# Layer 1 of a four-layer scan network: delta·u·B by plain multiplies for two of four pairs of states

## The chip, the core and the metric

The kernel runs on one core of a Trainium2 chip. The metric is the device time of one execution in microseconds (us). The engines have the short names of the profile: PE is TensorE, DVE is VectorE, ACT is ScalarE, POOL is GpSimd, and SP is the queue that issues most DMAs. All data are 32-bit floats.

## What is computed

The reference applies four layers to an image batch x of shape (4, 64, 64, 192). Only layer 1 is touched by the change. It runs four "mamba" blocks: over rows, rows reversed, columns, columns reversed. Each block treats every line of 64 pixels as a sequence of its own, with 384 channels d and 16 states n:

```
u      = silu(conv1d(in_proj(x)))                  # 4 taps, along the line
dt,B,C = x_proj(u)                                 # B, C: 16 values a pixel
delta  = softplus(dt_proj(dt) + bias)
h      = exp(delta * A[d,n]) * h + delta * u * B[n]     # along the line, h = 0 at its start
y[d]   = sum over n of h * C[n]
out    = out_proj((y + u * D) * silu(z))
```

Layers 0 and 3 are scans of the same kind over whole images, with a state carried on; layer 2 is a Toeplitz product by matmuls.

## The kernel before

**Chunks and units.** Layer 1 is cut into 128 jobs ("chunks"): 4 directions, 4 images, 8 chunks of T = 512 pixels (8 lines). A chunk has 384 channels, which are 6 groups g of 64, and 16 states, which are 4 pairs p: a tile of 128 partitions holds 64 channels twice, for the lower and the upper 8 states, and 2 x 512 columns hold two states of each half. So a unit (t, p, c) with g = 2t + c covers 64 channels and four states in one tile of 128 x 1024, and a chunk has 24 units: three tiles t, each with the eight (p, c) of the list `TWO` (L29).

**One unit.** `feed` (L304) makes the two inputs of the scan two units ahead (`AHEAD` = 2): delta·u·B, and dA = exp(delta·A) by two activations on ACT (L347). `scan` (L350) runs one `tensor_tensor_scan` on DVE (L357), and POOL multiplies h by C (L369) into hc. `collect` (L372) sums over states on PE by a matmul with `fold`, two units (c = 0 and 1) at a time, into y. When the last pair of a tile has been collected, `add` (here `gated`, L762) does y + uD on DVE and the product with z on POOL.

**delta·u·B in two ways.** For most units PE forms it: the transposed delta·u (`dtuT`) is the weight, and the moving operand is a set of diagonal matrices that carry B; eight matmuls (sixteen records in the trace) a unit at L324 write a PSUM tile b. The diagonals of one pair are 16 activations of 128 x 128 on ACT (L282), spread over four steps. Units listed in `direct`, in layer 1 both c of pair 3, need no diagonals: `spread` (L291) multiplies delta·u (tile `dtu2`) by a broadcast B (tile `bbc`) on POOL, three units ahead (`EARLY` = 3), into bs in SBUF (one buffer). For such a unit dA goes into the PSUM tile b instead of a fixed SBUF tile, and a copy (L335) first sets the start of each line in it to zero. PSUM has two buffers of b, so the work of `feed` for unit i + 2 that writes b waits for the scan of unit i.

**Order.** `run_jobs` (L104) emits, for each unit i, `feed` of i + 2, `scan` of i, `spread` of i + 3, one waiting `collect`, and then the steps that are due at i. The steps of a later chunk's preparation are placed by hand in `when` and `steps` (L784 to L789), counted in units from that chunk's start; minus 24 is one chunk earlier. So in the middle of a chunk's 24 units ACT has its table switches for `input_of` (L738, silu of u), `gate` (L752, silu of z) and `finish` (softplus) of later chunks. `plan` (L146) places the loads: tiles c (broadcast C), `bbc`, `both` (delta) and `dtu2` are fetched 12 units before their first use, or, where the buffer is still in use, a few units after its last one (`behind`: 2 in layer 1); diagonals 10 units before, or 3 after. A C tile is kept for a whole chunk, for all three t. The framework that lowers the program may shift instructions of one engine against each other, so the queues follow this order only roughly.

Of the kernel before, what the change touches and what calls it, by code (L numbers as in the profile page):

```python
# [7 lines left out]
F32 = mybir.dt.float32  # L8
# [11 lines left out]
T = 512  # L20
# [10 lines left out]
LAST = 2  # L31
LEAD = 12
LEAD_DIAG = 10
D1, PD, KD = 576, 96, 6
# [2 lines left out]
class Kernel:  # L37
# [66 lines left out]
    def run_jobs(self, jobs, pools):  # L104


        G = jobs[0]["DI"] // 64
        order = []
        for t in range(-(-G // 2)):
            order += [(t, *one) for one in (TWO if 2 * t + 1 < G else ONE)]  # L110
        units = [(k, *one) for k in range(len(jobs)) for one in order]
        per = len(order)
        steps = {}
        for k, job in enumerate(jobs):
            for at, step in self.prepare(job, pools) + job["steps"]:
                steps.setdefault(k * per + at, []).append(step)
        for at, load in self.plan(jobs, order, pools):
            steps.setdefault(at, []).append(load)
        start, end = min(steps), max(len(units) + 3, max(steps) + 1)
        waiting = []  # L120
        for i in range(min(start, -EARLY), end):
            if 0 <= i + AHEAD < len(units):
                k, t, p, c = units[i + AHEAD]
                self.feed(jobs[k], t, p, c, pools)
            todo = waiting[:1]
            if 0 <= i < len(units):
                k, t, p, c = units[i]
                self.scan(jobs[k], t, p, c, pools)
            if 0 <= i + EARLY < len(units):
                k, t, p, c = units[i + EARLY]  # L130
                if c in jobs[k]["direct"].get(p, ()):
                    self.spread(jobs[k], t, p, c, pools)
            if 0 <= i < len(units):
                if (i + 1) % 2 == 0:
                    waiting += [(units[i][0], [one[1:] for one in units[i - 1 : i + 1]], n) for n in range(2)]


            if todo:
                k, two, n = waiting.pop(0)
                self.collect(jobs[k], two, n, pools)  # L140
                if n and two[1][1] == LAST:
                    jobs[k]["add"](two[0][0])
            for step in steps.get(i, []):
                step()

    def plan(self, jobs, order, pools):  # L146


        uses, ready = {}, {}
        for k, job in enumerate(jobs):  # L150
            job["cbc"], job["bbc"], job["diag"], job["both"], job["dtu2"] = {}, {}, {}, {}, {}
            when = {name: k * len(order) + at for name, at in job["when"].items() if isinstance(at, int)}

            near = 2 if job["carry"] is not None else 5
            dtu = when["finish"] + 3 if job["carry"] is not None else when["store"] + 5
            for j, (t, p, c) in enumerate(order):
                i, g = k * len(order) + j, 2 * t + c
                direct = c in job["direct"].get(p, ())
                reads = [("c", p, i, when["project"] + 5), ("both", g, i - AHEAD, when["finish"] + near)]
                if direct:  # L160
                    reads += [("bc", p, i - EARLY, when["project"] + 5), ("dtu2", g, i - EARLY, dtu)]
                else:
                    reads.append(("diag", p, i - AHEAD, when["turn_b"] + 5))
                for name, key, at, after in reads:
                    first, _ = uses.setdefault(name, {}).get((k, key), (at, at))
                    uses[name][k, key] = first, at
                    ready[name, k] = after
        loads = []
        for name, of in uses.items():
            bufs, turn = pools["bufs"][name], sorted(of, key=of.get)  # L170
# [120 lines left out]
    def spread(self, job, t, p, c, pools):  # L291

        g = 2 * t + c
        b = pools["work"].tile([128, 2 * T], F32, name="bs", bufs=1)
        if job["carry"] is None:
            by = lambda one: one.rearrange("p (h n l) -> p h n l", h=2, n=2)
            dtu = job["dtu2"][g].rearrange("p (h l) -> p h l", h=2).unsqueeze(2).broadcast_to([128, 2, 2, 256])
        else:
            by = lambda one: one.rearrange("p (n l) -> p n l", n=2)
            dtu = job["dtu2"][g].unsqueeze(1).broadcast_to([128, 2, T])  # L300
        self.nc.gpsimd.tensor_mul(by(b), dtu, by(job["bbc"][p]))  # L301
        job["bs"][t, p, c] = b

    def feed(self, job, t, p, c, pools):  # L304

        nc = self.nc
        w, rev, g = job["w"], job["rev"], 2 * t + c
        lines = job["carry"] is None
        direct = c in job["direct"].get(p, ())
# [59 lines left out]
        nc.gpsimd.tensor_mul(hc, h, job["cbc"][p])  # L369
        job["done"][t, p, c] = hc  # L370

    def collect(self, job, units, n, pools):  # L372
# [5 lines left out]
        if first == 0 and n == 0:  # L378
# [12 lines left out]
    def neg_exp(self, A):  # L391
# [97 lines left out]
    def ss2d_scan(self, pre, u_d, y_d, P, NT, ways, A, dtb):  # L489
# [3 lines left out]
        with (  # L493
# [17 lines left out]
                for g in range(DI // 64) for p in range(PAIRS)  # L511
            }
            when = {
                3: dict(load=-33, project=-29, turn_b=-27, step_size=(-21, -19, -17), finish=-15,
                        turn=(-13, -11, -9), direct={3: (1,)}),
                2: dict(load=-25, project=-21, turn_b=-19, step_size=(-17, -16), finish=-14,
                        turn=(-9, -8), direct={3: (0, 1)}),
            }[NT]
            direct = when["direct"]

            for k, (col, rev) in sorted(enumerate(ways), key=lambda one: one[1]):
# [7 lines left out]
                for c in range(NCH - 1, -1, -1) if rev else range(NCH):  # L529
# [28 lines left out]
                    if rev:  # L558
# [1 line left out]
                            steps.append((8 * t + 2, lambda t=t, earlier=earlier: earlier(t)))  # L560
                    job.update(
                        P=P, NT=NT, DI=DI, k=k, w=w, rev=rev, carry=carry, first=first, add=add, y={}, fed={},
                        done={}, bs={}, when=when, steps=steps, direct=direct,
                    )
                    jobs.append(job)
            self.run_jobs(jobs, pools)
# [64 lines left out]
    def mamba(self, x_in):  # L631
# [73 lines left out]
    def mamba_job(self, pw, pin, mm, i, begin, rev, w, x, done, both_w, c, fixed, zero):  # L705
# [89 lines left out]
        return job  # L795

# [309 lines left out]
```

## Time and profile before

| what | us |
|---|---|
| median of 3 runs (lowest, highest) | 31818.84 (31812.0, 31833.96) |
| the profiled execution's own time | 31794.9 |
| its span, first to last instruction | 31793.1 |
| layer 1's scans, from the first to the last (read from the trace) | 11042 to 22315 |
| busy over the span: PE, DVE, ACT, POOL | 28311, 22475, 23362, 22678 |

Busy time is the time in which an engine has at least one instruction under way. For PE it contains the latency of pipelined matmuls, so it is no measure of how full PE is. In a group of the profile, the first number after the bar is the busy time, the second the mean of one instruction in ns; then comes the idle time of the engine just before these instructions and what ended it. A time divided by 128 below is a mean per chunk of layer 1.

### The profile page before, as it was taken

The numbers are of one execution on the slowest core, as the hardware profiler recorded it, in microseconds if no ns is written. First come the engines' busy times: TensorE is split into PE (matmuls) and PEld (weight loads), VectorE is DVE, ScalarE is ACT, GpSimd is POOL, SyncE is SP. The second block draws the span as 40 slices with busy tenths as digits, with TensorE's granted clock in tenths as the row PEclk, the third lists the DMA queues.
The fourth block names the chain that finished last, engine by engine and source line by source line (L and its number), as shares of the span: only waits on it lengthen the run. The fifth ranks groups of instructions, "written<-read, shape, count | busy, mean of one in ns | idle before, by whom it ended". The sixth has DMA issues, their size and how long they took to land. (4 is left out here: it accounts for less than half of the span.)

```text
span 31793.1 us, 449637 instructions
## 1 busy us (share of the span) xinstructions
PE 28311.3 (89%) x162840; PEld 13772.2 (43%) x162840; DVE 22474.8 (71%) x16587; ACT 23362.1 (73%) x50239; POOL 22678.0 (71%) x9755
## 2 busy tenths in 40 slices
PE   8997998999899699999999999999588988888888
PEld 4453554454445344444444444444355343434344
DVE  7887887788788677777777777777433267676767
ACT  7885885887688488888888888888133287878788
POOL 6884885888488488888888888888000086767777
PEclk9998999999999899999999999999788999999999
DMA  3333333333333423233333333333533444444444
GB/s 101 100 97 110 99 97 107 103 98 98 109 100 97 135 93 93 93 97 98 98 98 96 95 95 95 98 98 99 132 72 72 109 129 120 128 124 125 124 124 124
DMA packets 1565670, 3326.87 MB, mean 105 GB/s; under 512 B 343781, under 2 KB 356438, under 8 KB 1546934
## 3 DMA queue, kind: packets, MB, share of 16 engines
q1 hardware_dynamic: 1403702, 3021.19, 34.7%
q10 hardware_dynamic: 159744, 276.91, 2.6%
q8 instruction: 1289, 21.12, 0.3%
q14 instruction: 935, 7.66, 0.1%
HBM read 2137.94 MB, written 656.08 MB: 88 GB/s over the span
## 5 line engine op out<-in xcount | busy, mean ns | idle before, releaser
L369 POOL TENSOR_TENSOR hc<-h,c 128x1024 f32<-128x1024 f32 x7680 | 18189.2, 2384 | 3115.9 <-DVE h L364 1317.7
L324 PE MATMUL b<-diag,dtuT 128*64 128x256 f32 x98304 | 12805.9, 391 | 800.1 <-DVE h L364 679.9
L324 PEld LDWEIGHTS b<-diag,dtuT 128*64 128x64 f32 x98304 | 7507.3, 140 | 6835.9 <-issue 3091.1
L387 PE MATMUL y<-hc,fold 128*64 128x512 f32 x30720 | 8995.0, 598 | 587.4 <-POOL hc L369 572.6
L364 DVE TENSOR_TENSOR_SCAN h<-dA,carry,b 128x512 f32<-128x512 f32 x6720 | 8195.0, 1264 | 1805.9 <-PE b L324 1134.3
L347 ACT ACTIVATE dA<-both,A 128x512 f32<-128x512 f32 (+1 forms) x12288 | 8279.8, 711 | 203.0 <-DVE h L357 182.0
L357 DVE TENSOR_TENSOR_SCAN h<-dA,b 128x1024 f32<-128x1024 f32 x2304 | 5251.7, 2284 | 2047.7 <-PE b L324 883.2
L282 ACT ACTIVATE diag<-ident,bt 128x128 f32<-128x128 f32 x20480 | 6527.3, 391 | 124.5 <-ACT b L347 86.1
L301 POOL TENSOR_TENSOR bs<-dtu,bc 128x1024 f32<-128x1024 f32 x1536 | 3638.4, 2369 | 1479.7 <-DMA c<-bc_dram 1087.9
L387 PEld LDWEIGHTS y<-hc,fold 128*64 128x64 f32 x30720 | 2497.6, 138 | 2981.7 <-POOL hc L369 1262.0
L441 POOL MEMSET pad<- 128x13068 f32 (+1 forms) x8 | 73.4, 9177 | 3977.5 <-DMA inw<-in_L_in_w 3004.7
L347 ACT ACTIVATE b<-both,A 128x504 f32<-128x504 f32 (+1 forms) x3072 | 2078.1, 676 | 412.7 <-DVE h L364 379.8
L357 DVE TENSOR_TENSOR_SCAN h<-b,bs 128x1024 f32<-128x1024 f32 x768 | 1754.1, 2284 | 659.6 <-ACT b L347 391.2
L367 ACT COPY carry<-h 128x2 f32<-128x2 f32 x4608 | 851.4, 185 | 1367.1 <-DVE h L364 1165.5
L364 DVE TENSOR_TENSOR_SCAN h<-b,carry,bs 128x512 f32<-128x512 f32 x1344 | 1638.0, 1259 | 105.7 <-POOL hc L369 95.3
L364 DVE TENSOR_TENSOR_SCAN h<-dA,b 128x512 f32<-128x512 f32 x960 | 1112.9, 1205 | 436.2 <-ACT dA L347 175.8
L347 ACT ACT_TABLE_LOAD x1018 | 1306.1, 1283 | 15.0 <-ACT b L335 0.3
L730 PE MATMUL in_ps<-xn,in_w 96*128 96x512 f32 x1536 | 933.4, 738 | 329.4 <-DMA xn<-m_row 177.8
L747 DVE SCALAR_TENSOR_TENSOR u<-in_ps,conv_w,u 128x504 f32<-128x504 f32 (+2 forms) x1152 | 835.7, 725 | 460.3 <-ACT u L742 438.6
L233 DVE TENSOR_TENSOR dtu<-delta,u 128x1536 f32<-128x1536 f32 (+1 forms) x256 | 611.4, 2388 | 758.2 <-ACT delta L232 602.9
L242 PEld LDWEIGHTS dtu_ps<-ident,dtu 128*128 128x128 f32 (+1 forms) x4096 | 422.1, 142 | 875.7 <-issue 569.3
L730 PE MATMUL z_ps<-xn,in_w 96*128 96x512 f32 x1536 | 761.7, 618 | 0.0
(155 smaller groups left out, 22077.8 us busy)
## 6 DMA issues: line engine op xcount, KB each, us to landing
c<-bc_dram SPq DMA_DIRECT2D x3072, 256.0 KB
both<-delta SPq DMA_DIRECT2D x2048, 128.0 KB
bc<-bc_dram SPq DMA_DIRECT2D x768, 256.0 KB
both<-delta_dram SPq DMA_DIRECT2D x768, 256.0 KB
dtu<-dtu_dram SPq DMA_DIRECT2D x768, 256.0 KB
dtu<-dtu SPq DMA_DIRECT2D x1280, 128.0 KB
L_y<-out ACTq DMA_DIRECT2D x512, 256.0 KB
u<-L_u SPq DMA_DIRECT2D x160, 768.0 KB
```

The source lines that it names most:

```text
L233: (nc.gpsimd if job["carry"] is None else nc.vector).tensor_mul(job["dtu"], delta, job["u"])
L282: nc.scalar.activation(to, self.ident, AF.Copy, scale=of)
L301: self.nc.gpsimd.tensor_mul(by(b), dtu, by(job["bbc"][p]))
L324: nc.tensor.matmul(to, job["dtuT"][:, k, g * 64 : (g + 1) * 64], job["diag"][p][:, k, 2 * q : 2 * q + 2, :], start=True, stop=True,)
L347: nc.scalar.activation(to[n], of, AF.Exp, scale=w["A"][:, g, 2 * p + n : 2 * p + n + 1])
L357: nc.vector.tensor_tensor_scan(h[:, way], dA[:, way], b[:, way], 0.0, ALU.mult, ALU.add)
L364: nc.vector.tensor_tensor_scan(hn[:, n, way], dA[:, n, way], by_n[:, n, way], start, ALU.mult, ALU.add)
L367: nc.scalar.copy(carry[g, p], hn[:, :, 0 if rev else T - 1])
L369: nc.gpsimd.tensor_mul(hc, h, job["cbc"][p])
L387: nc.tensor.matmul(y[c * 64 : (c + 1) * 64, :], self.fold, of, start=first == 0 and n == 0, stop=last == LAST and n == 1)
L730: nc.tensor.matmul(ps, w["in_w"][:, k, to + t * P : to + (t + 1) * P], job["xn"][:, k, :], start=k == 0, stop=k == KC - 1,)
L747: nc.vector.scalar_tensor_tensor(u[:, :, to], ps[:, :, of], tap(3 - j), u[:, :, to], ALU.mult, ALU.add)
```

## The change

In layer 1, pair 1 becomes direct too: its six units of a chunk get delta·u·B by a multiply on DVE, pair 3's six on POOL as before. The other two pairs keep the diagonals and PE. A new list `LINES` puts the units so that matmul units and direct units alternate (0, 3, 2, 1, 0, 3, 2, 1). Since the first and last units of a tile now have other pairs, `collect` is told by `ends` whether it opens or closes y. bs gets a second buffer in layer 1, `bbc` a third, the diagonals go from four buffers to three and are rebuilt two units behind the last use instead of three. The hand-placed steps of layer 1 move by up to one unit, and the third `turn` (transposes of delta·u) by six. Layers 0 and 3 keep their units, order and steps; only the form of `direct` changes there.

```diff
+LINES = [(0, 0), (3, 1), (2, 0), (1, 1), (0, 1), (3, 0), (2, 1), (1, 0)]
...
-            order += [(t, *one) for one in (TWO if 2 * t + 1 < G else ONE)]
+            order += [(t, *one) for one in (jobs[0]["turns"] if 2 * t + 1 < G else ONE)]
...
-                if c in jobs[k]["direct"].get(p, ()):
+                if (p, c) in jobs[k]["direct"]:
                     self.spread(jobs[k], t, p, c, pools)
...
+                    tile = units[i][:2]
+                    ends = [j < 0 or j >= len(units) or units[j][:2] != tile for j in (i - 2, i + 1)]
...
-                        at = max(at, of[turn[j - bufs]][1] + 3)
+                        at = max(at, of[turn[j - bufs]][1] + pools["behind"])
...
-        b = pools["work"].tile([128, 2 * T], F32, name="bs", bufs=1)
+        b = pools["work"].tile([128, 2 * T], F32, name="bs", bufs=2 if job["carry"] is None else 1)
...
-        self.nc.gpsimd.tensor_mul(by(b), dtu, by(job["bbc"][p]))
+        job["direct"][p, c].tensor_mul(by(b), dtu, by(job["bbc"][p]))
...
-        t, first, _ = units[0]
-        last = units[1][1]
+        t, (first, last) = units[0][0], ends
...
-                y[c * 64 : (c + 1) * 64, :], self.fold, of, start=first == 0 and n == 0, stop=last == LAST and n == 1
+                y[c * 64 : (c + 1) * 64, :], self.fold, of, start=first and n == 0, stop=last and n == 1
...
-        bufs = dict(c=4, bc=2, diag=4, both=4, dtu2=2)
+        bufs = dict(c=4, bc=3, diag=3, both=4, dtu2=2)
...
-        when = dict(project=-24, turn_b=-22, step_size=(-20, -18, -17), finish=-15, turn=(-10, -7, -3), store=-11)
+        when = dict(project=-23, turn_b=-21, step_size=(-19, -18, -17), finish=-15, turn=(-9, -7, 3), store=-11)
...
-        steps += [(-48, load)] + each(input_of, (-45, -32, -29)) + each(gate, (-6, -4, -2)) + each(out, (32, 35))
+        steps += [(-48, load)] + each(input_of, (-45, -33, -29)) + each(gate, (-5, -3, -1)) + each(out, (33, 35))
...
-            add=gated, when=when, steps=steps, begin=start_lines if begin else None, direct={3: (0, 1)},
-            zero=zero,
+            add=gated, when=when, steps=steps, begin=start_lines if begin else None, zero=zero, turns=LINES,
+            direct={(p, c): nc.vector if p == 1 else nc.gpsimd for p in (1, 3) for c in range(2)},
```

More of the change, by code (lines that the diff above doesn't have):

```diff
@@ L30 @@
 ONE = [(0, 0), (3, 0), (1, 0), (2, 0)]
-LAST = 2
+LINES = [(0, 0), (3, 1), (2, 0), (1, 1), (0, 1), (3, 0), (2, 1), (1, 0)]
 LEAD = 12
@@ L134, in run_jobs @@
                 if (i + 1) % 2 == 0:
-                    waiting += [(units[i][0], [one[1:] for one in units[i - 1 : i + 1]], n) for n in range(2)]
+                    tile = units[i][:2]
+                    ends = [j < 0 or j >= len(units) or units[j][:2] != tile for j in (i - 2, i + 1)]
+                    waiting += [(units[i][0], [one[1:] for one in units[i - 1 : i + 1]], n, ends) for n in range(2)]
             if todo:
-                k, two, n = waiting.pop(0)
-                self.collect(jobs[k], two, n, pools)
-                if n and two[1][1] == LAST:
+                k, two, n, ends = waiting.pop(0)
+                self.collect(jobs[k], two, n, ends, pools)
+                if n and ends[1]:
                     jobs[k]["add"](two[0][0])
@@ L157, in plan @@
                 i, g = k * len(order) + j, 2 * t + c
-                direct = c in job["direct"].get(p, ())
+                direct = (p, c) in job["direct"]
                 reads = [("c", p, i, when["project"] + 5), ("both", g, i - AHEAD, when["finish"] + near)]
@@ L308, in feed @@
         lines = job["carry"] is None
-        direct = c in job["direct"].get(p, ())
+        direct = (p, c) in job["direct"]
         wide = pools["b"].tile([128, 2 * T], F32, name="b")
@@ L370, in scan, with collect @@
         job["done"][t, p, c] = hc
-    def collect(self, job, units, n, pools):
+    def collect(self, job, units, n, ends, pools):
         nc = self.nc
-        t, first, _ = units[0]
-        last = units[1][1]
+        t, (first, last) = units[0][0], ends
         units = sorted(units, key=lambda one: one[2])
-        if first == 0 and n == 0:
+        if first and n == 0:
             job["y"][t] = pools["y"].tile([128, T], F32, name="y")
@@ L514, in ss2d_scan @@
                 3: dict(load=-33, project=-29, turn_b=-27, step_size=(-21, -19, -17), finish=-15,
-                        turn=(-13, -11, -9), direct={3: (1,)}),
+                        turn=(-13, -11, -9), direct={(3, 1): nc.gpsimd}),
                 2: dict(load=-25, project=-21, turn_b=-19, step_size=(-17, -16), finish=-14,
-                        turn=(-9, -8), direct={3: (0, 1)}),
+                        turn=(-9, -8), direct={(3, 0): nc.gpsimd, (3, 1): nc.gpsimd}),
             }[NT]
@@ L562, in ss2d_scan @@
                         P=P, NT=NT, DI=DI, k=k, w=w, rev=rev, carry=carry, first=first, add=add, y={}, fed={},
-                        done={}, bs={}, when=when, steps=steps, direct=direct,
+                        done={}, bs={}, when=when, steps=steps, direct=direct, turns=TWO,
                     )
```

## The prediction

> **What bounds the kernel now.** The change touches only layer 1, so I first took the busy times of its stretch, then its groups, the waits, and one boundary between chunks in order of time. The stretch (columns: length, then busy us of each engine with its instructions, granted clock, DMA):
>
> ```profile
> core 0: us, PE busy (x) PEld busy (x) DVE busy (x) ACT busy (x) POOL busy (x), PEclk, DMA share, GB/s
> 11042.00:22315.00 11273.00, 10639.38 (x57216) 4655.00 (x57216) 8074.15 (x4717) 9197.28 (x16939) 9871.01 (x4357) 0.97 0.31 96
> ```
>
> Over 128 chunks: a chunk takes 88.1 us, and in it POOL is busy 77.1, ACT 71.9, DVE 63.1 and PE 83.1. PE's figure is latency: in the order of time a unit's group of sixteen b matmuls starts at 15004.80, its y matmuls at 15006.52, the next b group at 15007.38, so b costs 1.72 us and y 0.86. 18 x 1.72 + 24 x 0.86 = 51.6; some 42 records of 512 columns (in, z, o, xd), 0.43 apart, add 18, the small ones some 4: an estimate of 74. The fullest engine is therefore POOL, with 11.0 us idle a chunk. The groups:
>
> ```profile
> L369 POOL TENSOR_TENSOR hc<-h,c 128x1024 f32<-128x1024 f32 x3070 | 7217.0, 2368 | 1396.5 <-DVE h L357 1254.5 <-PE b L324 97.7 <-DMA c<-bc_dram 30.4
> L357 DVE TENSOR_TENSOR_SCAN h<-dA,b 128x1024 f32<-128x1024 f32 x2304 | 5251.7, 2284 | 2047.7 <-PE b L324 883.2 <-ACT dA L347 779.7 <-POOL hc L369 228.4
> L282 ACT ACTIVATE diag<-ident,bt 128x128 f32<-128x128 f32 x6096 | 1950.6, 390 | 98.6 <-ACT b L347 86.1 <-DMA dtu<-dtu_dram 12.5
> L357 DVE TENSOR_TENSOR_SCAN h<-b,bs 128x1024 f32<-128x1024 f32 x768 | 1754.1, 2284 | 659.6 <-ACT b L347 391.2 <-POOL bs L301 201.6 <-POOL dtu L233 58.1
> ```
>
> POOL's idle time is h that comes late; h is late a chunk by 6.9 us for PE's b, 6.1 for ACT's dA, 3.1 for ACT's direct dA. Where ACT's 6.1 falls shows at a boundary of chunks. DVE, POOL, then part of ACT:
>
> ```profile
> 15041.41 2.29 DVE L357 TENSOR_TENSOR_SCAN h<-dA,b 128x1024 f32<-128x1024 f32 x1 [2.69 <-ACT dA L347]
> 15047.09 2.29 DVE L357 TENSOR_TENSOR_SCAN h<-dA,b 128x1024 f32<-128x1024 f32 x1 [3.40 <-ACT dA L347]
> ```
> ```profile
> 15043.77 2.36 POOL L369 TENSOR_TENSOR hc<-h,c 128x1024 f32<-128x1024 f32 x1 [2.55 <-DVE h L357]
> 15049.52 2.37 POOL L369 TENSOR_TENSOR hc<-h,c 128x1024 f32<-128x1024 f32 x1 [3.40 <-DVE h L357]
> ```
> ```profile
> 15042.39 0.70 ACT L347 ACTIVATE dA<-both,A 128x504 f32<-128x504 f32 x1
> 15043.10 1.28 ACT L755 ACT_TABLE_LOAD   x1
> 15044.39 0.60 ACT L755 ACTIVATE z<-z_ps 128x512 f32<-128x512 f32 x1
> 15044.99 1.28 ACT L347 ACT_TABLE_LOAD   x1
> 15046.29 0.72 ACT L347 ACTIVATE dA<-both,A 128x504 f32<-128x504 f32 x1
> ```
>
> The two halves of one unit's dA stand 3.9 us apart, with a switch to silu and back between. From 15025 to 15047 ACT never rests: four such trips, two silus of u, three of z and about 18 diagonals fall together, and the scans, then POOL, starve for 6 of POOL's 11 us.
>
> **What the Trainium skill says.** "SBUF — State Buffer", section "SBUF: two separate sides": a DVE instruction with two SBUF inputs and a GpSimd instruction exclude each other for whole instructions. The scans escape, having one input in PSUM; the new DVE multiply doesn't. Layer 3's delta·u multiply on DVE is a twin, and agrees:
>
> ```profile
> 26644.28 2.23 DVE L233 TENSOR_TENSOR dtu<-delta,u 96x1024 f32<-96x1024 f32 x1
> ```
> ```profile
> 26643.07 5.67 POOL L369 TENSOR_TENSOR hc<-h,c 128x1024 f32<-128x1024 f32 x2
> 26649.05 4.72 POOL L369 TENSOR_TENSOR hc<-h,c 128x1024 f32<-128x1024 f32 x2 [0.31 <-DVE h L364]
> ```
>
> DVE starts 1.2 us into POOL's first multiply, waits for its end and needs 2.23 us; POOL's pair needs 5.67 instead of 4.72. "Perfetto Trace Analysis", section "Identifying the Most-Contended Engine": occupancy is fair for Vector, Scalar and GpSimd, not for matmuls; the 83.1 against 74 agree.
>
> **The change part by part, a chunk.**
>
> *PE* loses 6 x 1.72 = 10.3 us: 74 becomes 64. This shortens nothing by itself; it can take away the 6.9 us for which scans wait for b. Matmul and direct units now alternate, so b has two scans' time (4.6 us) rather than one (2.28, against b and y of 2.58).
>
> *ACT* loses 16 diagonals, 6.2 us, and gains six zero copies of L335 at 0.17: 71.9 becomes 66.7. But half the units now put dA into PSUM, so ACT stops twice as often for a scan to free b, with everything behind it in its queue: 589.9 us in the stretch, 4.6 a chunk, perhaps 9. While ACT has time to spare that costs nothing.
>
> *DVE* gains six multiplies of 1024 columns. Alone, the row of L606 with a broadcast operand has 1204 ns; beside POOL the twin's mean in layer 3 is 1746; at worst the wait is a whole POOL multiply, 1.20 + 2.37 = 3.57. So 6 x 1.75 = 10.5, at worst 21.4; 63.1 becomes 73.6, at worst 84.5. I take the mean, since layer 3's POOL is about as full. Behind a waiting multiply stand the next scans, and for them POOL.
>
> *POOL* keeps six spreads, and loses 5.67 - 4.72 = 0.95 at each DVE multiply: 5.7, or nothing where it is idle anyway. 77.1 becomes 82.8.
>
> *Moved steps.* Silu trips now sit at 15, 19, 21, 23 of the chunk before instead of 16, 18 to 20, 22; one fewer falls into the dense stretch: 2 x 1.28 + 0.72 = 3.3. The third turn's copy (0.58) leaves it, and the three of pair 1's diagonals that were inside, 1.2; zero copies return 0.3. So ACT's jam shrinks by some 4.7 us, from both sides between 1 (if the queue packs them as tightly) and 6. Project, turn_b, out: one unit, same work, hidden by ACT's idle first half. Diagonals of pair 2 still fall on 20 to 23, since they wait for their buffer: nothing gained there.
>
> *Loads.* SP issues two more for B of pair 1, about 0.5 us each, 0.26 MB a chunk on DMA engines 31% busy: nothing. C tiles now have four units between last and next use instead of five or seven, and are fetched after two of them. An issue takes 1.1 us for the pair, their packets end some 3 us later; POOL has three hc and a spread, 9.5 us, meanwhile. Zero; without that cover, up to 3 us a chunk. dtu2 has four units, and the second bs buffer keeps DVE's multiply from waiting for a scan: zero.
>
> **Sum.** POOL's floor is 82.8. Idle at the boundary: 6.0 + about 0.9 just after, less 4.7, leaves 2.2. The other 4.1 us stem mostly from late b and half of it should go: 2.0. 82.8 + 4.2 = 87.0 a chunk, against 88.1: 1.1 x 128 = 137 us. The profiled execution took 31794.9 (span plus 2), so 31,658; the median of the runs stands 24 higher: **31,680 us**, 0.4% faster.
>
> **Rivals.**
> 1. *DVE becomes the bound (slower).* Its in-order queue holds multiplies that wait for POOL, and the scans behind them. DVE now idles 25.0 us a chunk. If only the boundary's 4.7 and half of b's 6.9 go, 16.8 stay: 63.1 + 10.5 + 16.8 = 90.4, +2.3 x 128 = +300: 32,115. It decides from 14.5 us of left-over waits on (88.1 - 73.6); my forecast leaves 13.4, so the margin is thin. For it: half the direct units' dA is on ACT's critical side. Against it: some 4.6 us of DVE's waits are for POOL, and overlap the lock.
> 2. *No change.* POOL's 5.7 us of lock eat exactly the idle time saved: idle falls from 11.0 to 5.3. 31,820.
> 3. *A larger gain.* With PE and ACT both relieved, POOL idles only 1.5 us: 84.3, -3.8 x 128 = -483: 31,336. For it: POOL is dense already for half of each chunk, and the lock makes its backlog longer.
> 4. *ACT's jam stays* because the queue packs the silus as before; POOL idles 8 and more: 90.8, +350: 32,170.
>
> **How the numbers follow.** A measurement of this kernel tells 0.2%, 64 us or 0.5 us a chunk. Forecast, 85.7 to 87.5 a chunk: 0.45, its own range 31,520 to 31,750; gain beyond that (3): 0.13; no change (2): 0.17; DVE bound (1): 0.16; jam (4) or late C tiles: 0.09. Faster 0.58, same 0.17, slower 0.25. The range runs from most of case 3 to the centre of 1: 31,400 to 32,090.
>
> **What would show it.** Right: L324 with two thirds of its records; POOL's hc and spreads up by some 0.9 us at each DVE multiply, which takes 1.7 to 2.4; idle time of hc down from 1396 us to some 550; scans' wait for PE b near zero. Wrong: the DVE multiply's mean near 3.5; POOL idle over 5.3 us a chunk; hc waiting for c; dA waits at the boundary as long as now. A changed layer 0 or 3 would break the whole sum.

## The result, and the profile after

The changed kernel takes 33,058.94 us (median of 4 runs, 33,052.46 to 33,065.25) against 31,822.5 us of the kernel before beside it: a ratio of 1.0388, interval 1.037 to 1.0406. It is 1,236 us slower; the prediction said 137 us faster. All of it lies in layer 1: its stretch is 12,542 us long in the profile after, and was 11,273 before. The stretch after the change, in the columns of the prediction (length, busy us of each engine with its instructions, granted clock of PE, DMA):

```profile
core 0: us, PE busy (x) PEld busy (x) DVE busy (x) ACT busy (x) POOL busy (x), PEclk, DMA share, GB/s
11052.00:23594.00 12542.00, 10494.37 (x44961) 4145.35 (x44962) 9157.73 (x5485) 8892.36 (x15796) 10607.55 (x4358) 0.93 0.29 91
```

Over 128 chunks: 98.0 us a chunk, where it was 88.1. POOL is busy 82.9 of them; the prediction's floor was 82.8. But it is idle for 15.1, not for 4.2. So the work was costed rightly, and the idle time was not. The groups of layer 1 after (lines have moved by two; busy time, mean ns, then the idle time before them and what ended it):

```profile
L371 POOL TENSOR_TENSOR hc<-h,c 128x1024 f32<-128x1024 f32 x3071 | 7935.1, 2600 | 1319.6 <-DVE h L359 1242.1 <-DMA c<-bc_dram 21.2 <-PE y L388 20.7
L388 PE MATMUL y<-hc,fold 128*64 128x512 f32 x12280 | 4714.0, 675 | 1786.6 <-POOL hc L371 1782.9
L359 DVE TENSOR_TENSOR_SCAN h<-b,bs 128x1024 f32<-128x1024 f32 x1536 | 3505.3, 2282 | 996.8 <-ACT b L349 841.8 <-issue 150.2 <-ACT diag L284 1.9
L359 DVE TENSOR_TENSOR_SCAN h<-dA,b 128x1024 f32<-128x1024 f32 x1536 | 3492.6, 2274 | 993.1 <-PE b L326 628.5 <-POOL hc L371 215.9 <-ACT dA L349 134.7
L303 DVE TENSOR_TENSOR bs<-dtu,bc 128x1024 f32<-128x1024 f32 x768 | 1231.0, 1603 | 21.9 <-DMA dtu<-dtu_dram 9.0
L766 POOL TENSOR_TENSOR z<-z,u 128x512 f32<-128x512 f32 x383 | 486.6, 1271 | 612.6 <-DVE u L765 612.6
```

hc's mean is up from 2368 to 2600 ns (the lock), the multiply takes 1603 ns, and the scans' wait for ACT's dA, 779.7 us before, is down to 134.7. New is the second row: y's matmuls now stop for POOL. The waits of the same stretch (total, times, longest):

```profile
PEld y L388 <- POOL hc L371: 2715.3, 1219, 5.7
ACT b L337 <- DVE h L359: 2071.9, 1085, 9.1
PE y L388 <- POOL hc L371: 1782.9, 785, 4.8
POOL hc L371 <- DVE h L359: 1242.1, 840, 4.2
DVE u L765 <- PE y L388: 1103.0, 349, 6.8
```

Before, PE's y waited 183 us for hc, now 1,783; ACT's zero copy waited 590 us for a scan, now 2,072; gated (L765) waited 3 us for y, now 1,103. (PEld rows are PE's weight loads.) Engines that had been relieved now stand still, and hold what is queued behind them. One such case in order of time, PE first, then DVE, then POOL:

```profile
15050.32 3.68 PE L388 MATMUL y<-hc,fold 128*64 128x512 f32 x6 [3.98 <-POOL hc L371]
15053.92 0.61 PE L221 MATMUL b_ps<-ident,xd 16*128 16x16 f32 x4
15054.46 2.53 PE L326 MATMUL b<-diag,dtuT 128*64 128x256 f32 x16
```
```profile
15047.69 2.26 DVE L359 TENSOR_TENSOR_SCAN h<-dA,b 128x1024 f32<-128x1024 f32 x1
15049.90 2.29 DVE L359 TENSOR_TENSOR_SCAN h<-b,bs 128x1024 f32<-128x1024 f32 x1
15052.23 1.43 DVE L303 TENSOR_TENSOR bs<-dtu,bc 128x1024 f32<-128x1024 f32 x1
15057.13 2.29 DVE L359 TENSOR_TENSOR_SCAN h<-dA,b 128x1024 f32<-128x1024 f32 x1 [3.48 <-PE b L326]
```
```profile
15047.91 2.35 POOL L371 TENSOR_TENSOR hc<-h,c 128x1024 f32<-128x1024 f32 x1 [0.98 <-DVE h L359]
15059.50 4.68 POOL L371 TENSOR_TENSOR hc<-h,c 128x1024 f32<-128x1024 f32 x2 [1.32 <-DVE h L359]
```

POOL's hc ends at 15050.26, and only then can PE start y. The next b (unit 4 of the chunk) had its PSUM tile from 15049.95 on, when the scan of unit 2 ended, but it is queued behind that y and starts at 15054.46. Its scan therefore stops for 3.48 us behind the multiply, and then POOL for 1.32. POOL, running late, has made itself wait. The case is typical: such a stop of y stands there in 127 of the 128 chunks, of 3.98 us in most, and the scan of unit 4 alone has 386 of the 628 us for which scans wait for PE's b.

The stop itself ends only 0.4 us after the tile is free. What holds b for the other 4.1 us is the work of y (and of b_ps), which now falls there, at half the clock. PE's granted clock, the third number from the end of each line, while y ran, while b ran, and later:

```profile
15050.30:15054.00 3.70, 3.68 (x7) 0.84 (x8) 3.32 (x2) 2.06 (x5) 3.70 (x2) 0.50 0.16 46
15054.00:15057.10 3.10, 3.10 (x21) 2.02 (x22) 0.00 (x0) 2.54 (x5) 3.10 (x2) 0.73 0.35 110
15060.00:15068.00 8.00, 8.00 (x43) 3.37 (x41) 7.12 (x5) 5.07 (x9) 8.00 (x4) 1.00 0.14 48
```

Six records of y took 3.68 us, where four took 1.08 at 15058.24; b took 2.53, where it took 1.95 at 15061.16. An estimate from the clocks shown: at full clock this b would have been ready 2.7 us earlier (3.7 x 0.50 + 3.1 x 0.27). Why the clock fell there no run shows. In the 127 chunks PE's granted clock between the end of that stop and the start of unit 4's scan was 0.63 in the mean.

### The profile page after: what moved, and what is told of

Its sections match the earlier page's. It is cut to its first block, busy times and chain, and to the rows that moved or that the text cites. A ratio compares the mean times of both kernels' runs of the same rounds, so it can differ in the third digit from the quotient of the medians.

```text
span 33063.3 us, 425389 instructions
## 1 busy us (share of the span) xinstructions
PE 28152.3 (85%) x150552; PEld 13252.1 (40%) x150552; DVE 23560.3 (71%) x17355; ACT 23061.0 (70%) x49089; POOL 23406.5 (71%) x9755
## 5 line engine op out<-in xcount | busy, mean ns | idle before, releaser
L371 POOL TENSOR_TENSOR hc<-h,c 128x1024 f32<-128x1024 f32 x7680 | 18898.4, 2476 | 3048.3 <-DVE h L366 1342.4
L326 PE MATMUL b<-diag,dtuT 128*64 128x256 f32 x86016 | 11599.9, 394 | 937.7 <-DVE h L366 679.9
L388 PE MATMUL y<-hc,fold 128*64 128x512 f32 x30720 | 10323.3, 631 | 2178.3 <-POOL hc L371 2174.6
L326 PEld LDWEIGHTS b<-diag,dtuT 128*64 128x64 f32 x86016 | 6817.0, 141 | 6080.7 <-issue 2931.0
L349 ACT ACTIVATE dA<-both,A 128x512 f32<-128x512 f32 (+1 forms) x10752 | 7211.7, 710 | 36.7 <-DVE h L359 30.8
L284 ACT ACTIVATE diag<-ident,bt 128x128 f32<-128x128 f32 x18432 | 5948.3, 390 | 26.7 <-issue 0.5
L359 DVE TENSOR_TENSOR_SCAN h<-b,bs 128x1024 f32<-128x1024 f32 x1536 | 3505.3, 2282 | 996.8 <-ACT b L349 841.8
L359 DVE TENSOR_TENSOR_SCAN h<-dA,b 128x1024 f32<-128x1024 f32 x1536 | 3492.6, 2274 | 993.1 <-PE b L326 628.5
L349 ACT ACTIVATE b<-both,A 128x504 f32<-128x504 f32 (+1 forms) x4608 | 3122.2, 678 | 428.8 <-DVE h L366 381.5
L303 DVE TENSOR_TENSOR bs<-dtu,bc 128x1024 f32<-128x1024 f32 x768 | 1231.0, 1603 | 21.9 <-DMA dtu<-dtu_dram 9.0
L765 DVE SCALAR_TENSOR_TENSOR u<-u,D,y 128x512 f32<-128x512 f32 x384 | 286.5, 746 | 1107.6 <-PE y L388 1107.6
```

What stands on the lines that cost most here:

```text
L284: nc.scalar.activation(to, self.ident, AF.Copy, scale=of)
L303: job["direct"][p, c].tensor_mul(by(b), dtu, by(job["bbc"][p]))
L326: nc.tensor.matmul(to, job["dtuT"][:, k, g * 64 : (g + 1) * 64], job["diag"][p][:, k, 2 * q : 2 * q + 2, :], start=True, stop=True,)
L349: nc.scalar.activation(to[n], of, AF.Exp, scale=w["A"][:, g, 2 * p + n : 2 * p + n + 1])
L359: nc.vector.tensor_tensor_scan(h[:, way], dA[:, way], b[:, way], 0.0, ALU.mult, ALU.add)
L388: nc.tensor.matmul(y[c * 64 : (c + 1) * 64, :], self.fold, of, start=first and n == 0, stop=last and n == 1)
```

## The experiments

Kernels of one batch ran beside the same runs of the kernel before; its medians in the five batches, in the order of this section, were 31,842.6, 31,850.4, 31,816.8, 31,839.1 (y_first and y_borrow) and 31,842.8 us (y_before and y_later).

### Gated's place in DVE's queue (Theory Q)

After the change gated stands behind the first scan of the next tile (behind the second in one tile of three), and waits there for y with the scans behind it; before, it stood behind the fourth (the third in one tile of three). Three kernels move it back, behind the second, third and fourth scan; two_order puts the old order of units and the old step times under the new operations. All compute what the changed kernel does.

```diff
-                    jobs[k]["add"](two[0][0])
+                    add = lambda job=jobs[k], t=two[0][0]: job["add"](t)
+                    if jobs[k]["carry"] is None and i + 1 < len(units):     # late0: 0, late2: 2
+                        steps.setdefault(i + 1, []).append(add)
...
+            self.queue(gate, self.last_scan)      # an order within DVE's queue, no semaphore
```

> The changed kernel, with one thing moved: on DVE the product y + uD that closes a tile (gated) is held behind the second scan of the next tile instead of the first. Theory Q (queue): in the changed kernel this product waits 8.6 us a chunk for PE's y, since it stands one to two scans too early in DVE's queue, and the scans behind it and POOL's z wait with it. One scan (2.3 us) later, the waits of 4.9, 3.1 and 1.0 us per tile become about 2.6, 0.8 and 0: 5 us less a chunk, 640 us: 32,300 to 32,550. Theory L (lock and direct units): the time went to the six multiplies on DVE, to the port that they share with POOL and to ACT's stops for PSUM; the wait for y only shows slack. Then 32,900 to 33,100.

> As late0, but the product is held behind the third scan of the next tile, where it stands in the kernel before; nothing else changes on DVE. Theory Q: its wait for y falls from 8.6 us a chunk below 1, POOL's wait for it from 4.8 to below 1, and the time to 31,800 to 32,300. Theory L: 32,900 to 33,100, and the idle time turns up at the scans instead.

> As late1, but held behind the fourth scan; the queues of DVE and POOL shift in other places too (the multiply of pair 1 moves by a scan). Theory Q: no wait for y left to win, so within 150 us of late1, 31,800 to 32,400. Theory L: 32,900 to 33,150.

Measured: late0 33,237.6 us (1.0445 [1.043, 1.0461]), late1 33,253.2 (1.0453 [1.0437, 1.0469]), late2 33,507.6 (1.0532 [1.0514, 1.055]). The changed kernel is at 1.0388. In late1 gated hardly waits for y (4.6 us, once), and POOL is still idle for 16.6 us a chunk. Its waits in layer 1:

```profile
PEld y L392 <- POOL hc L375: 3108.0, 1191, 7.3
PE y L392 <- POOL hc L375: 2198.8, 1012, 6.4
ACT b L341 <- DVE h L363: 1930.8, 956, 7.7
POOL hc L375 <- DVE h L363: 1716.2, 890, 4.9
DVE h L363 <- ACT b L353: 1248.2, 602, 3.8
```

The 1,103 us that gated had waited have moved to the waits of y, hc and the scans. Theory Q fell: that wait was a symptom. The three times also lie above Theory L's ranges, by 138 to 358 us.

```diff
-        when = dict(project=-23, turn_b=-21, step_size=(-19, -18, -17), finish=-15, turn=(-9, -7, 3), store=-11)
+        when = dict(project=-24, turn_b=-22, step_size=(-20, -18, -17), finish=-15, turn=(-10, -7, -3), store=-11)
...
-            add=gated, when=when, steps=steps, begin=start_lines if begin else None, zero=zero, turns=LINES,
+            add=gated, when=when, steps=steps, begin=start_lines if begin else None, zero=zero, turns=TWO,
```

> The changed kernel with the unit list TWO and the step times of the kernel before; pair 1 is still multiplied on DVE, with the new buffers. In its queue the product y + uD stands behind the second, third and third scan of the next tile. Theory Q: little wait for y, 31,900 to 32,400. Theory L: the six multiplies and the twelve direct units are all there, so 32,800 to 33,200.

Measured: 33,303.6 us (1.0468 [1.0452, 1.0484]), above both ranges. Putting the old order back is no help, but this run doesn't clear the alternation: the DVE multiply now waits 1,553 us for the transfer of dtu2, 9 us in the changed kernel. two_nomult, further down, has no multiply and says more.

### The multiply and its lock

no_mult leaves the DVE multiply out: pair 1's scans read a fixed tile of zeros, so a fourth of layer 1's delta·u·B is missing from its result. before_mult and before_reduce add six DVE instructions a chunk to the kernel before, each held between a scan of pair 1 and the next scan: a multiply with two inputs in SBUF, which writes over the dA tile that the scan has read, or a reduction of the same size with one, which writes one column of a small tile.

```diff
+        if job["direct"][p, c] is self.nc.vector:        # no_mult
+            job["bs"][t, p, c] = job["blank"]
+            return
```
```diff
+        if carry is None and p == 1:                     # before_mult
+            self.extra = nc.vector.tensor_mul(by(dA), by(job["cbc"][p]), by(job["cbc"][p]))
...
+            self.extra = nc.vector.tensor_reduce(most, by(job["cbc"][p]), axis=mybir.AxisListType.XY, op=ALU.max)   # before_reduce
```

> The changed kernel without the six multiplies on DVE: pair 1's scans read a fixed tile of zeros, so that a fourth of layer 1's delta u B is left out; its twelve direct units, their loads, diagonals and step times stay, and so does the order of DVE's other work. Theory L (port): the loss is the multiplies' lock on the port shared with POOL and their DVE time; without them 31,000 to 31,700. Theory D (direct units): the loss is that half the units now have dA in PSUM, so that ACT may write it only after the scan two units before; then still 32,300 to 33,000.

> The kernel before, with nothing direct added, plus six multiplies of 128 x 1008 on DVE a chunk, each right behind a scan of pair 1 and ahead of the next scan; they take two SBUF inputs (C twice) and write over the dA tile that the scan has finished with. Theory L: most of the loss comes back, 32,600 to 33,200. Theory D: at most POOL's own lost time, 0.95 us each, 730 us, and less where POOL is idle: 31,950 to 32,550.

> As before_mult, at the same places in the queue, but a maximum over the same 1008 columns of C with one SBUF input, about 1.1 us each, which should not contend for the port. Theory L: DVE has 25 us to spare a chunk, so 31,850 to 32,150; what before_mult costs beyond it is the port. If DVE's time or its place in the queue were the cause, both would cost the same.

Measured: no_mult 32,519.4 us (1.0212 [1.0195, 1.0229]), before_mult 32,215.0 (1.0118 [1.0103, 1.0133]), before_reduce 31,746.3 (0.9968 [0.9956, 0.998]). The groups of before_mult in layer 1, then those of before_reduce:

```profile
L377 POOL TENSOR_TENSOR hc<-h,c 128x1024 f32<-128x1024 f32 x3071 | 7808.4, 2558 | 1091.5 <-DVE h L358 1039.3 <-DMA c<-bc_dram 4.1 <-PE b L325 0.6
L375 DVE TENSOR_TENSOR dA<-c 128x1008 f32<-128x1008 f32 x768 | 1908.8, 2485 | 17.6
```
```profile
L379 POOL TENSOR_TENSOR hc<-h,c 128x1024 f32<-128x1024 f32 x3071 | 7227.7, 2375 | 1305.7 <-DVE h L358 1240.3 <-DMA c<-bc_dram 44.9 <-DVE most L376 5.7
L376 DVE TENSOR_REDUCE most<-c 128x1 f32<-128x1008 f32 x768 | 907.9, 1182 | 0.0
```

The place in DVE's queue costs nothing: six more instructions of 1182 ns there, and POOL's hc stays at 2375 ns (the time even lies 104 us below Theory L's range; why is open). With the second input in SBUF hc rises to 2558 ns. This is the exclusion of the Trainium skill, "SBUF — State Buffer", section "SBUF: two separate sides", and these two rows agree with it; the expectations call it the port that the two engines share. In time the multiply costs 365 us in the kernel before (32,215.0 less 31,850.4), and 540 us in the changed one (33,058.9 less 32,519.4). The first of these is not all the lock's: ACT's dA waits 545 us for the multiply to be done with the dA tile, and each multiply holds DVE 1.3 us longer than a reduction. So the lock is real, and the multiply with all that it brings is less than half of the loss: no_mult does no multiply, gives PE and ACT less work than before, and takes 669 us more. Its waits in layer 1 have the same new head:

```profile
PEld y L391 <- POOL hc L374: 2485.5, 1272, 5.5
PE y L391 <- POOL hc L374: 1547.8, 722, 4.6
ACT b L340 <- DVE h L362: 1411.5, 984, 5.4
DVE u L770 <- PE y L391: 1316.6, 316, 6.8
```

psum_mult keeps the multiply and its two inputs in SBUF, but spares ACT six PSUM tiles a chunk: the multiply writes b into the PSUM tile one unit ahead of its scan, and pair 1's dA stays in the fixed SBUF tiles.

```diff
-        b = pools["work"].tile([128, 2 * T], F32, name="bs", bufs=2 if job["carry"] is None else 1)
+        near = job["direct"][p, c] is self.nc.vector
+        b = job["fed"][t, p, c][0] if near else pools["work"].tile([128, 2 * T], F32, name="bs", bufs=1)
```

> The changed kernel, but pair 1's multiply writes delta u B into the PSUM tile, one unit ahead of its scan, and dA of these units goes into the fixed SBUF tiles as for matmul units. So ACT waits for PSUM in six units of 24, as before, and the multiply's two SBUF inputs stay. Theory L: within 300 us of the changed kernel, 32,750 to 33,350. Theory D: 31,600 to 32,400.

Measured: 33,898.9 us (1.0647 [1.0631, 1.0663]); POOL is idle 23.4 us a chunk. That is above both ranges, so it decides nothing between the theories, and it was not followed further.

### TensorE's queue (Theory Y) and ScalarE's PSUM tiles (Theory Z)

The framework orders each queue itself, and its order on PE had changed with the operations. Numbering b by its unit and y by the second unit of its pair, with .0 and .1 for the two halves, the compiled queues of one chunk begin so (a half consists of two matmuls, and stands where its first one does):

```
before:  b0 b1 b3 y1.0 b4 y1.1 b6 y3.0 b7 y3.1 b8 y5.0 b9 y5.1 y7.0 b11 ...
after:   b0 b2 y1.0 y1.1 b4 y3.0 y3.1 b6 y5.0 b8 y5.1 b10 y7.0 y7.1 y9.0 b12 ...
y_after: b0 b2 b4 y1.0 y1.1 b6 y3.0 y3.1 b8 y5.0 y5.1 b10 y7.0 y7.1 b12 ...
```

In the changed kernel y of units 2 and 3 stands ahead of b of unit 6, the next b in turn; before, its halves stood behind b of units 6 and 7. In the traces, of the eight y records of a pair of units, as a rule all eight of units 0 and 1 run ahead of b4 and six of units 2 and 3 ahead of b6; before, two and none. The shift is uneven: ahead of b10 no y is early. y_after puts y back behind the next b, and gated behind the third scan; y_nomult does it to no_mult. In the trace of y_after a few matmuls of the projections in_ps and z_ps stand at other places among the b too.

```diff
+            if job["carry"] is None:
+                self.queue(sums, self.last_b)     # sums: y's matmul; last_b: the b matmul emitted last
```

> The changed kernel with two orders pinned, and nothing else: in TensorE's queue the matmuls that sum hc into y stand behind the b matmuls written before them (y of a pair of units behind b of the unit three later, as they mostly stood before the change), and gated stands behind the third scan of the next tile. Theory Y (TensorE stops at y for GpSimd's hc with the next b queued behind it, so GpSimd may not fall behind VectorE by a unit without the scan stopping too): most of the 5.2 us a chunk that no multiply explains comes back, 32,000 to 32,600 us, and the wait of y on hc falls from 1,783 us to below 600. Theory Z (ScalarE: with twelve units in alternation it must fill one of two PSUM tiles in the time of a single scan, and stops 16 us a chunk for it): TensorE's order is not the cause, 33,000 to 33,400 us.

> The kernel no_mult (pair 1's scans read a fixed tile of zeros, so a fourth of layer 1's delta u B is left out) with the two pins of y_after. Theory Y: 31,000 to 31,900 us, no slower than the kernel before. Theory Z: 32,300 to 32,700 us, as no_mult was (32,519).

Measured: y_after 32,179.6 us (1.0113 [1.0098, 1.0128]), y_nomult 32,015.3 (1.0065 [1.0048, 1.0082]). y_after is inside Theory Y's range: 880 of the 1,236 us are back, by an order alone (y's, with the few projections that moved along). Against late1, which has gated in the same place and PE's order of the changed kernel, the difference is 1,074 us. y_nomult gained 504 us and missed Theory Y's range by 115: something is left. The waits of y_after in layer 1:

```profile
ACT b L341 <- DVE h L363: 1625.2, 1106, 6.4
PE b L330 <- DVE h L363: 1257.1, 811, 6.2
DVE h L363 <- ACT b L353: 1133.4, 450, 4.9
POOL hc L375 <- DVE h L363: 709.5, 381, 4.1
PE y L392 <- POOL hc L375: 441.2, 335, 3.9
```

y's wait is down from 1,783 to 441 us, hc's from 1,242 to 710. PE now stops at b for the scan that frees the tile (1,257 us), which does little harm, since another scan runs before the one that needs this b (scans wait 190 us for PE's b). What rises to the top is the scans' wait for ACT's b. A direct unit's dA goes into one of the two PSUM tiles, so ACT can begin only when the scan two units back has ended. It then has a single scan, 2.28 us, for a zero copy and two activations (0.17 + 2 x 0.68 = 1.5 us), whatever else is queued. That is now asked of it twelve times a chunk. borrow takes six of them away from no_mult: pair 1's dA goes to the fixed SBUF tiles, and its scan reads as b the PSUM tile of the unit before. two_nomult tries no_mult in the old order.

```diff
+        borrow = direct and job["direct"][p, c] is self.nc.vector
+        wide = self.wide if borrow else pools["b"].tile([128, 2 * T], F32, name="b")
...
-            if direct:
+            if direct and not borrow:
                 dA = wide
```

> The kernel no_mult with one thing changed: for pair 1 ScalarE writes dA into the fixed SBUF tiles that TensorE's units use, not into a PSUM tile, and the scan reads as b the PSUM tile of the unit before it (so a fourth of layer 1's result is wrong, and nothing is multiplied for it). ScalarE then has six PSUM tiles to fill a chunk, as before the change, not twelve; TensorE's and GpSimd's work is that of no_mult. Theory Z: the 5.2 us a chunk go, 31,500 to 31,950 us, and ScalarE's stops at the zero columns fall from 16 us a chunk to below 6. Theory Y: nothing of it changes y's place, 32,300 to 32,600 us.

> The kernel no_mult in the order of units and with the step times of the kernel before (TWO: the direct units stand at 2, 3, 4 and 5 of each eight, not at every second one). It says whether the order by alternation or the removal of work from TensorE and ScalarE costs the 5.2 us a chunk. If the alternation does: 31,400 to 31,950 us. Theory Z: four direct units in a row leave ScalarE the same single scan for each and no TensorE unit between them, so it is no better, 32,400 to 33,000 us. Theory Y says 32,300 to 32,900 us, since y is queued ahead of the next b in either order.

Measured: borrow 32,322.2 us (1.0158 [1.0143, 1.0174]), two_nomult 32,323.0 (1.016 [1.0144, 1.0175]). Neither comes back to the time before, as Theory Z and the alternation would have had it; Theory Y's ranges hold both. In borrow PE's y still waits 1,441 us for hc. So ScalarE's tiles alone are not the cause. Nor are borrow's 197 us theirs alone, since the queue of PE moved with the edit (two y records of units 0 and 1 run ahead of b4, eight in no_mult). Putting the old order back in two_nomult gained 196 us, of 669: most of the loss without the multiply isn't the alternation's. y_borrow has both remedies, borrow's edit and the pins of y_after.

> The kernel borrow (no multiply for pair 1; its dA in the fixed SBUF tiles, its b the PSUM tile of the unit before, so a fourth of layer 1's result is wrong) with the two pins of y_after. Borrow took 32,322 us and the pins alone, on no_mult, 32,015 us. If the two queues are two separate costs, TensorE's stops at y and ScalarE's late PSUM tiles: both go, 31,200 to 31,800 us, below the kernel before, and VectorE's wait for ScalarE's b falls from 2,003 us to below 600. If they are one cost seen in two places: 31,900 to 32,100 us.

Measured: 31,554.3 us (0.9909 [0.9892, 0.9926]), below the kernel before and in the range for two separate costs. But the scans' wait for ACT's b is 1,447 us, down from 2,003 in y_nomult, where below 600 was expected:

```profile
DVE h L369 <- ACT b L359: 1447.3, 443, 4.4
DVE h L369 <- POOL hc L381: 1092.1, 512, 4.4
ACT b L347 <- DVE h L369: 923.2, 496, 9.7
POOL hc L381 <- DVE h L369: 798.1, 435, 4.1
```

So the cost of the tiles is shown by the time (461 us against y_nomult), and hardly by that wait. It needn't be ACT's alone: a borrowed tile serves two units, so PE's b too finds its tile free earlier. DVE has room for its 11.3 us a chunk: it stops another 8.5 for h buffers that POOL has not read yet, being ahead of POOL. What counts is POOL's wait for h, 6.2 us a chunk. The two costs are also not independent: one at a time the remedies gave 504 and 197 us, together 965.

### The order alone, in the kernel before

y_first puts y one place earlier in PE's queue of the kernel before. In its trace y is early at every b, where the change left some out, and no other matmul has another place among the b; gated stands behind the third scan, one earlier than before in two tiles of three, and never waits there. y_before pins y behind b of the unit three later. By its trace this moves one y matmul a chunk, and not three as expected, from ahead of b of unit 4 to behind it. y_later moves all y one place back. None changes an operation.

```diff
+                for k, two, n in waiting[:2]:            # y_first: ahead of feed, and b pinned behind the last y
+                    self.collect(jobs[k], two, n, pools)
...
+                self.queue(sums, self.last_b)            # y_before; y_later: collect one unit later as well
```

> The kernel before, with TensorE's queue put as the change left it: the matmuls that sum hc into y stand one place earlier, ahead of the b of the unit three later (y of units 2 and 3 ahead of b of unit 6, where before has them ahead of and behind b of unit 7); gated's place is left behind the third scan, and no operation is added or taken away. Theory Y: the order alone costs hundreds of us, 32,100 to 32,700, with the wait of y on hc up from 183 us to above 700. If that order only hurts beside the change's other parts (Theory Z, or both together): 31,750 to 31,950 us.

> The kernel before with y's matmuls pinned behind the b of the unit three later. Of its queue this moves one thing: the first y of each tile goes from ahead of b of unit 4 to behind it, three times a chunk. Theory Y: the same or a little faster, 31,600 to 31,900 us. A chance of a version that beats both kernels.

> The kernel before with y's matmuls pinned one place later than they stood (y of units 2 and 3 behind b of units 7 and 8), which also puts gated one or two scans later. Theory Y, if later is always better: 31,400 to 31,750 us. If the order of before was late enough, and only an early y hurts: 31,750 to 32,200 us, since hc and gated are then kept longer.

Measured: y_first 32,305.6 us (1.0146 [1.013, 1.0161]), y_before 32,309.6 (1.0145 [1.0128, 1.0162]), y_later 32,849.4 (1.0315 [1.03, 1.0331]). An early y, with gated a scan earlier, costs 466 us: the time is in Theory Y's range. The sign that was to go with it failed: y waits 579 us for hc, where above 700 was expected (183 before). The scans' wait for b rose more, from 883 to 1,735 us. Part of y_first's loss is the very stop; PE, then DVE:

```profile
14793.98 1.65 PE L396 MATMUL y<-hc,fold 128*64 128x512 f32 x5 [2.23 <-POOL hc L378]
14794.90 0.74 PE L331 MATMUL b<-diag,dtuT 128*64 128x256 f32 x2
14795.42 1.06 PE L396 MATMUL y<-hc,fold 128*64 128x512 f32 x1
14795.44 4.97 PE L331 MATMUL b<-diag,dtuT 128*64 128x256 f32 x27
```
```profile
14799.43 4.46 DVE L366 TENSOR_TENSOR_SCAN h<-dA,b 128x1024 f32<-128x1024 f32 x2 [6.27 <-PE b L331]
```

Another part is a wait of 6.6 us of DVE for ACT's u later in the same chunk, which is not for y (967 us in all for such waits, 412 before). And y_before, expected to be harmless, missed its range by 410 us. Its PE and DVE at the moved b, and then PE of the kernel before at the same place:

```profile
14768.64 2.07 PE L738 MATMUL in_ps<-xn,in_w 96*128 96x512 f32 x2 [6.55 <-DMA xn<-m_row]
14770.64 3.60 PE L324 MATMUL b<-diag,dtuT 128*64 128x256 f32 x16
```
```profile
14774.40 2.29 DVE L357 TENSOR_TENSOR_SCAN h<-dA,b 128x1024 f32<-128x1024 f32 x1 [9.38 <-PE b L324]
```
```profile
14609.79 1.24 PE L324 MATMUL b<-diag,dtuT 128*64 128x256 f32 x9
14611.98 1.08 PE L387 MATMUL y<-hc,fold 128*64 128x512 f32 x4
14616.11 3.78 PE L730 MATMUL in_ps<-xn,in_w 96*128 96x512 f32 x4 [3.06 <-DMA xn<-m_row]
14619.83 2.99 PE L324 MATMUL b<-diag,dtuT 128*64 128x256 f32 x16
```

With y behind it, the framework let b of unit 4 slip behind the first half of the projection in_ps, which waits for a transfer. That b's tile was free from 14762.7 on, when the scan before ended; it waited with the projection, and its scan stopped for 9.38 us; in the kernel before b of unit 4 (first line) is out by then. So it is not y as such. Whatever waits at the head of PE's queue holds the b behind it, be it for hc or for a transfer. The Trainium skill says the underlying thing in "PSUM — Partial Sum Buffer", section "Engine vs sequencer instructions": matmuls start and complete in program order. The cuts above agree: b at 15054.46 started behind y, and b at 14770.64 behind in_ps, 4.5 and 7.9 us after its tile was free. A later y was no gain either, and missed both ranges; y_later also keeps gated back, and POOL there waits 684 us for PE's y and 903 us for c.

No version with the whole computation is better by more than before_reduce's 0.3%, and that one only adds useless reductions.

## Why the prediction was wrong

A table of means per chunk, in us, from layer 1's stretch of each profile (its length, POOL's busy time and the waits, divided by 128):

| | before | after | y_after | y_borrow |
|---|---|---|---|---|
| chunk | 88.1 | 98.0 | 91.0 | 86.1 |
| POOL busy | 77.1 | 82.9 | 82.7 | 76.9 |
| POOL idle | 11.0 | 15.1 | 8.3 | 9.3 |
| y waits for hc (PE) | 1.4 | 13.9 | 3.4 | 4.9 |
| scan waits for b (PE) | 6.9 | 4.9 | 1.5 | 0.8 |
| scan waits for b (ACT) | 3.1 | 6.6 | 8.9 | 11.3 |
| scan waits for dA (ACT) | 6.1 | 1.1 | 0.9 | 0.1 |

**POOL and DVE** were right: the lock's 5.7 us gave 82.9 for 82.8, and the multiply took 1603 ns for 1.75 us.

**The jam at the boundary** moved more than it shrank. By the traces the scans of a chunk's first three units waited 6.9 us for ACT before and none after, but those of units 19 to 23 waited 2.1 us and now wait 6.1. The table's last row falls by 5.0, near the forecast 4.7, only because a direct unit's dA is counted as b, one row up, and there are twice as many such units. The two rows together fall from 9.2 to 7.6 us. And the step "6.0 + about 0.9 just after, less 4.7, leaves 2.2" took all of the 4.7 off POOL's idle time, which did not follow: in no_mult, where the lock is absent, POOL is idle for 16.7 us a chunk.

**"The other 4.1 us stem mostly from late b and half of it should go: 2.0" is the step that failed.** It rested on b having two scans' time, as matmul and direct units alternate. But a direct unit takes one of the two PSUM tiles as well: b may begin only when the scan two units back has ended, and is due one scan later (in the case shown from 15049.95 to 15053.66, with the multiply between). And it looked at PE's load, not at its queue. The order there became y, then b, so b waits for POOL, whose lag the lock makes longer; without the lock, in no_mult, y still waits 1,548 us for hc. Scans' wait for PE's b, to come near zero, is 4.9 us a chunk. Idle time of POOL was predicted to be 4.2 and is 15.1; with y put back it is 8.3. The 1.72 us of a b are its work at full clock; what decides is when that work may start. The prediction named what is queued behind a waiting instruction on DVE and ACT, and never on PE.

**"While ACT has time to spare that costs nothing"** failed too. ACT's stops were put at perhaps 9 us a chunk and are 16.2, and six fewer PSUM tiles to fill gave 461 us once y was in its place.

**Zero for C tiles** was right: hc waits 21 us in all for c.

**The rivals.** The sign of rivals 1 and 4 was right; the mechanism of neither explains the loss. DVE, rival 1's bound, is busy 71.5 of 98.0 us. Of rival 4's jam most stayed (7.6 of 9.2 us), but at other units, and y_after, with 9.8 us of the same waits, got back 880 us. The range ended 969 us short, and no rival had a mechanism in PE's queue.

**The sum, as the runs have it.** From the changed kernel downwards: y put back, 880 us; then the multiply taken out, 164 (y_after to y_nomult); then six PSUM tiles less, 461 (y_borrow). What is left is 285 us below the kernel before: the gain from relieving PE and ACT, in a kernel that leaves pair 1's delta·u·B out. In another sequence the shares differ (multiply first 540, then y 504), so they are no fixed prices.

**What stays open.** Why the framework chose each order was not studied. The loss cannot be called one cause: y_first, y_before and y_later show that the kernel before loses 1.5 to 3% by moving matmuls in either direction, so a part of any change here may be the loss of a fortunate order. What the moved projections did in y_after, and what PE's half clock cost in all, no run separates. A remedy that keeps the computation and frees both the port and the PSUM tiles was not found.

## What to carry to other kernels

Relief of an engine should not be counted as a gain until its queue has been read: for the instruction that feeds the bottleneck, list what stands ahead of it and what each of those waits for, and ask whether removing neighbours lets the compiler pull a waiting instruction ahead. Where two buffers pass between engines, count how many units of each kind must be filled in the time of one step. And before believing a gain of a per cent, learn what a seemingly harmless shift does: here a pin that moved one y matmul a chunk, and let one b slip behind a projection, cost 1.5%.

## What was not expected of the hardware

The lock's price on POOL hardly depends on how long DVE has to wait. The two-input multiply's mean was 1603 ns in the changed kernel, 2145 in y_after and 2485 in before_mult (which has 1008 columns); POOL's busy time rose to 82.7 to 82.9 us a chunk in all three. The granted clock in layer 1 fell from 0.97 to 0.93 although PE had a fifth fewer matmuls: in the trace's record of the clock PE runs at half clock for 1,823 us of it, in 411 stretches, and for 696 us in 107 before. This doesn't go with the loss over the runs: y_after has 1,532 us at half clock and got back 880 us, and y_first has 621 and lost 466.
